# Ternary signs prepared during the offset stage, weights loaded behind the first image, and a first split in four parts

## The chip, the core and the metric

The kernel runs on one core of a Trainium2 chip. The time is device microseconds (us) from start to end. Engines: PE does matmuls (PEld is its weight load), DVE is the vector engine, ACT the scalar engine, POOL is GpSimd, SP issues most of the DMA transfers. PE's clock is granted by a throttle, 1.00 being full. A ratio is the mean time of one kernel's fast runs over that of the other's of the same rounds, so not quite the ratio of the medians that are quoted. Kernels are compared only within the same rounds.

## The reference, cut to what matters

Input is x, two images of 256 channels at 128 x 128, float32.

```python
x = x + L0(group_norm(x))        # three deformable branches, layer norms, GELU, an MLP
x = x + L1(group_norm(x))

def L1(x):                       # weight is (256, 256, 3, 3)
    max_val = max(abs(weight)); w_norm = weight / max_val
    delta = 0.05 * max(abs(w_norm))
    tern = where(w_norm > delta, 1, where(w_norm < -delta, -1, 0))
    wq = where(tern > 0, Wp * tern, where(tern < 0, Wn * tern, tern))
    return conv3x3(x, wq) + bias
```

The ternary weights depend on the inputs alone, not on any result of L0. They can be prepared at any time.

## The kernel before

Four stages follow one another. **Start**: image one is read for its group-norm statistics. **Offset stage** (`phase_a`, 64 groups of four rows over both images): normalise, transpose, convolve to offsets, write interpolation factors (hats). Image two's statistics run beside it. **Sampling stage** with its tail of norms and MLP; it ends with the last store to `x1d`. **Convolution** (`phase_c_signs`): signs in bf16, the image split into three bf16 parts whose sum is the float32 value, 4608 matmuls.

What the change touches:

```python
    def load(name, shape, src):                      # at the very start, 16 loads of weights
        tl = const.tile(shape, F32, name=name)
        nc.sync.dma_start(tl, src)                   # SP issues them before the image
        return tl
    ...
        for b in range(NB):                          # statistics of an image
            for c in range(KC):
                for g0 in range(0, NGRP, XT):
                    xt = ap.tile([P, XT * NG], F32, name="xt", tag="xt", bufs=3)   # ring of three, 1 MB each
                    nc.sync.dma_start(xt, ...)
                    for j in range(XT):
                        nc.vector.bn_stats(...)
            mean, rstd = group_norm(stats, f"gn1_{b}", gps)
            ...
            phase_a(b, ap, psum, k)
    ...
    def quantise(pool, signs=None):                  # in the convolution stage, before its groups
        wq = pool.tile([P, KC, 9, C], F32, ...)
        nc.sync.dma_start(wq, ...)                   # 2304 KB
        nc.vector.tensor_reduce(own, wq, ..., ALU.max, apply_absolute_value=True)
        nc.gpsimd.partition_all_reduce(m, own, ...)
        ...                                          # 13 operations on one column: the thresholds
        for k in range(KC):
            for tap in range(9):
                ts(up, w, pr, ALU.subtract, er, ALU.is_ge)
                ts(dn, w, pr, ALU.add, nc_, ALU.is_le)
                nc.vector.tensor_tensor(signs[:, k, tap, :], up, dn, ALU.subtract)
    ...
    def phase_c_signs(...):
        mean, rstd = group_norm(stats2[b], ...)      # at each image
        for g in range(H // RC):
            ...                                      # xl from x1d; xn normalised; D, four differences of rows
                left = D.rearrange("p i j w -> p (i j) w")
                for i in range(2):
                    part = xc[:, i, k, :, 1 : 1 + W]
                    nc.scalar.copy(part, left)       # 2048 elements at once
                    nc.vector.tensor_tensor(left if i == 0 else xc[:, 2, k, ...], left, part, ALU.subtract)
            for m in range(KC):
                ...                                  # 72 matmuls into four banks, then six DVE additions
```

Names in the profiles: xa is one group's rows of the image, loaded by ACT's queue and normalised by DVE; tpa are its transposes on PE; pz and po are the matmuls that lead to the offsets (offs); parts are the offsets cut into bf16 pieces, which PE transposes (pp) and multiplies to the hats (ph, hb). In the convolution D holds the differences of rows, cring the split image and pc the sums.

Of the kernel before, what the change touches and what calls it, by code (L numbers as in the profile page):

```python
# [9 lines left out]
F32 = mybir.dt.float32  # L10
# [57 lines left out]
def conv_preact_kernel(ctx: ExitStack, tc: tile.TileContext, t: dict, out: bass.AP):  # L68
# [19 lines left out]

    def load(name, shape, src):
        tl = const.tile(shape, F32, name=name)  # L90
        nc.sync.dma_start(tl, src)
        return tl

    gmask = load("gmask", [P, P], t["gmask"])
    convs = [
# [18 lines left out]

    def dram(name, shape):
        return [scratch.tile(shape, F32, name=f"{name}{b}", tag=f"{name}{b}") for b in range(NB)]
# [8 lines left out]
    yd = scratch.tile([3, C, HW], F32, name="yd")  # L125

# [33 lines left out]
    def phase_a(b, pool, psum, k):  # L160
# [160 lines left out]
        for g in range(NGRP):  # L321
            columns(g)
            while G < H // ZG and min(H - 1, G * ZG + ZG - 1 + max(DILS)) < (g + 1) * R:
                parts = offsets(G)
                for j in range(ZG // R):
                    make_hats(G * (ZG // R) + j, parts, j * R)
                G += 1

    with ExitStack() as actx:
# [18 lines left out]
        nc.sync.dma_start(k["wz"], t["wz"].rearrange("(k p) n -> p k n", p=P))  # L348
        nc.sync.dma_start(k["shift"], t["shift"])
        hatw = ap.tile([P, 2, NTAP * NH], F32, name="hatw32")  # L350
        nc.sync.dma_start(hatw, t["hatw"])
        nc.vector.tensor_copy(k["hatw"], hatw)
        pattern = ap.tile([P, NG], F32, name="pattern")
        nc.sync.dma_start(pattern[HALF : HALF + NPAT], t["pattern"])
        for pl in k["planes"]:
            nc.vector.tensor_copy(
                pl[HALF : HALF + NPAT, 1, :], pattern[HALF : HALF + NPAT]
            )
        for parts in k["parts"]:
            nc.vector.memset(parts, 0.0)  # L360
        XT = min(4, NGRP)
        for b in range(NB):
            stats = ap.tile([P, KC, NGRP, 6], F32, name=f"stats1_{b}", tag=f"stats1_{b}")
            for c in range(KC):
                for g0 in range(0, NGRP, XT):
                    xt = ap.tile([P, XT * NG], F32, name="xt", tag="xt", bufs=3)
                    nc.sync.dma_start(
                        xt,
                        x[b, c * P : (c + 1) * P].rearrange("p h w -> p (h w)")[
                            :, g0 * NG : (g0 + XT) * NG  # L370
                        ],
                    )
                    for j in range(XT):
                        nc.vector.bn_stats(stats[:, c, g0 + j, :], xt[:, j * NG : (j + 1) * NG])
            mean, rstd = group_norm(stats, f"gn1_{b}", gps)
            gn1.append((mean, rstd))

            nc.vector.tensor_scalar(negmean[b], mean, -1.0, None, ALU.mult)
            for c in range(KC):
                nc.vector.tensor_scalar(  # L380
                    convs[b][:, c, :], convs[b][:, c, :], rstd[:, c : c + 1], None, ALU.mult
                )
            phase_a(b, ap, psum, k)
# [8 lines left out]
    beyond = nc.values_load(flag[0:1, 0:1], min_val=0, max_val=1)  # L392

# [527 lines left out]
    def quantise(pool, signs=None):  # L921

        wq = pool.tile([P, KC, 9, C], F32, name="wq", tag="wq", bufs=1)
        nc.sync.dma_start(wq, t["l1w"].rearrange("(k p) t o -> p k t o", p=P))
        scale = []
        for name in ("wp", "wn"):
            s = pool.tile([P, 1], F32, name=name, tag=name, bufs=1)
            nc.sync.dma_start(s, t[name].partition_broadcast(P))
            scale.append(s)
        wp, wn = scale  # L930
        nc.vector.tensor_scalar(wn, wn, -1.0, None, ALU.mult)

        def col(name):
            return pool.tile([P, 1], F32, name=name, tag=name, bufs=1)

        own, m, mh, ml, pr, er, z, nc_ = (
            col(f"q_{i}") for i in ("own", "m", "mh", "ml", "pr", "er", "z", "nc")
        )
        nc.vector.tensor_reduce(
            own, wq.rearrange("p k t o -> p (k t o)"), AX.X, ALU.max, apply_absolute_value=True  # L940
        )
        nc.gpsimd.partition_all_reduce(m, own, P, bass.bass_isa.ReduceOp.max)  # L942



        def ts(dst, a, s1, op0, s2=None, op1=None):
            nc.vector.tensor_scalar(dst, a, s1, s2, op0, *(() if op1 is None else (op1,)))

        ts(mh, m, 4097.0, ALU.mult)
        nc.vector.tensor_tensor(ml, mh, m, ALU.subtract)  # L950
        nc.vector.tensor_tensor(mh, mh, ml, ALU.subtract)
        nc.vector.tensor_tensor(ml, m, mh, ALU.subtract)
        ts(pr, m, THR, ALU.mult)
        nc.vector.scalar_tensor_tensor(er, mh, THR_HI, pr, ALU.mult, ALU.subtract)
        nc.vector.scalar_tensor_tensor(er, mh, THR_LO, er, ALU.mult, ALU.add)
        nc.vector.scalar_tensor_tensor(er, ml, THR_HI, er, ALU.mult, ALU.add)
        nc.vector.scalar_tensor_tensor(er, ml, THR_LO, er, ALU.mult, ALU.add)
        nc.vector.scalar_tensor_tensor(er, m, THR_HALF_ULP, er, ALU.mult, ALU.add)

        ts(z, m, 0.0, ALU.is_equal)  # L960
        nc.vector.tensor_tensor(pr, pr, z, ALU.add)
        ts(nc_, er, -1.0, ALU.mult)
        for k in range(KC):
            for tap in range(9):
                w = wq[:, k, tap, :]
                up = pool.tile([P, C], F32, name="up", tag="up", bufs=1)
                ts(up, w, pr, ALU.subtract, er, ALU.is_ge)
                dn = pool.tile([P, C], F32, name="dn", tag="dn", bufs=1)
                ts(dn, w, pr, ALU.add, nc_, ALU.is_le)
                if signs is not None:  # L970
                    nc.vector.tensor_tensor(signs[:, k, tap, :], up, dn, ALU.subtract)  # L971
                    continue
                ts(up, up, wp, ALU.mult)
                nc.vector.scalar_tensor_tensor(w, dn, wn, up, ALU.mult, ALU.add)
        return wq

# [51 lines left out]
    def phase_c_signs(b, pool, psum, cring, signs, sums, wp, half):  # L1028
# [9 lines left out]
        JC = RC // 2  # L1038
        for g in range(H // RC):
# [4 lines left out]
            for k in range(KC):  # L1044
                nc.sync.dma_start(xl[:, k, rows, :], xv[:, k, lo:hi, :])
            xc = cring[g % len(cring)]
            for k in range(KC):
# [16 lines left out]
                left = D.rearrange("p i j w -> p (i j) w")  # L1064
                for i in range(2):
                    part = xc[:, i, k, :, 1 : 1 + W]
                    nc.scalar.copy(part, left)  # L1067
                    nc.vector.tensor_tensor(  # L1068
                        left if i == 0 else xc[:, 2, k, :, 1 : 1 + W], left, part, ALU.subtract
                    )  # L1070
            for m in range(KC):
                pc = psum.tile([P, 4, 512], F32, name="pc", tag="pc", bufs=2)

                for bank, t in ((0, 0), (1, 3), (2, 1), (3, 2)):
# [3 lines left out]
                    for j, (k, kx, i) in enumerate(todo):  # L1078
                        w = (
                            signs[:, k, (t // 3 * 2) * 3 + kx] if t % 3 == 0  # L1080
                            else sums[:, k, t - 1, kx]
# [30 lines left out]

    wpn = small.tile([P, 2], F32, name="wpn", tag="wpn", bufs=1)
    for i, name in enumerate(("wp", "wn")):
        nc.sync.dma_start(wpn[:, i : i + 1], t[name].partition_broadcast(P))
    eq = const.tile([P, 1], I32, name="eq")
    nc.vector.tensor_tensor(eq, wpn[:, 0:1], wpn[:, 1:2], ALU.is_equal)
    same = nc.values_load(eq[0:1, 0:1], min_val=0, max_val=1)

    with tc.If(same > 0) as cmp:  # L1120
        with ExitStack() as cctx:
# [10 lines left out]
            signs = cp.tile([P, KC, 9, C], BF16, name="signs")  # L1132
            quantise(cp, signs)

            sums = cp.tile([P, KC, 2, 3, C], BF16, name="sums")
            for k in range(KC):
                nc.vector.tensor_tensor(
                    sums[:, k, 0], signs[:, k, 0:3], signs[:, k, 6:9], ALU.add
                )
                nc.vector.tensor_tensor(  # L1140
                    sums[:, k, 1], sums[:, k, 0], signs[:, k, 3:6], ALU.subtract
                )
                nc.vector.tensor_tensor(  # L1143
                    sums[:, k, 0], sums[:, k, 0], signs[:, k, 3:6], ALU.add
                )
            half = cp.tile([P, 2], F32, name="half")
            for i in range(2):
                nc.vector.tensor_scalar(
                    half[:, i : i + 1], wpn[:, 0:1], 0.5 - i, None, ALU.mult
                )  # L1150
            for b in range(NB):
                phase_c_signs(b, cp, psum, cring, signs, sums, wpn[:, 0:1], half)
# [102 lines left out]
```

## Time and profile before

| | us |
|---|---|
| median of 3 runs | 7885.2 (7873.1 to 7889.1) |
| span of the profiled execution (timed at 7904.9) | 7903.1 |
| start, to the first pz matmul | 83.5 |
| offset stage, to the last hat (hb) | 874.7 |
| seam, to the first sampling matmul (pm) | 22.4 |
| sampling and tail, to the issue of the last x1d store | 5828.9 |
| convolution, to the end | 1093.6 |

The five stages add up to the span. The lengths come from first and last start times in the views by tile. A hat's end is that of its last DVE operation. From the page of the kernel before: the span; each engine's busy time, share and instruction count; and half of the convolution's matmuls (busy us, mean ns of one, then PE's idle time just ahead of them and what ended most of it).

```profile
span 7903.1 us, 115440 instructions
...
PE 7101.1 (90%) x37984; PEld 5421.9 (69%) x37984; DVE 6400.1 (81%) x13680; ACT 4514.7 (57%) x9350; POOL 715.1 (9%) x1292
...
L1083 PE MATMUL pc<-cring,signs 128*128 128x512 bf16 x2304 | 522.8, 386 | 56.1 <-DVE signs L971 23.6
```

PE is busy for 90% of the span. What a change can take away are the idle stretches, and the last line names one: PE waits in front of the convolution for signs. The shares over the span say nothing of the seams; those are read in the prediction.

### The profile page before, as it was taken

The page shows a single profiled execution, that of the slowest core. Times are in us where ns is not written, and L with a number is a line of the kernel's source. Part 1 is how long each engine was busy: PE and PEld are TensorE (multiplying, and loading weights), DVE is VectorE, ACT ScalarE, POOL GpSimd, SP SyncE. Part 2 cuts the span into 40 slices and gives each one's busy share as a digit, 9 for nine tenths or more (in the row PEclk, how much of TensorE's full clock was granted, in tenths as well). Part 3 has the DMA queues.
Part 4 walks back from the last instruction along what each step waited for, and adds up shares of the span by engine and source line. Part 5 has one row for each costly group of instructions (what it writes and reads, how often), then busy time and mean ns, then how long its engine had stood idle before and what let it go on. Part 6 is the DMA issues. An engine that isn't in the chain of part 4 may idle for free. (4 is left out here: it accounts for less than half of the span.)

```text
span 7903.1 us, 115440 instructions
## 1 busy us (share of the span) xinstructions
PE 7101.1 (90%) x37984; PEld 5421.9 (69%) x37984; DVE 6400.1 (81%) x13680; ACT 4514.7 (57%) x9350; POOL 715.1 (9%) x1292
## 2 busy tenths in 40 slices
PE   5999887899999999899988989999998999699999
PEld 2555577777887777777777777877787777344444
DVE  6666578888999889988688898898889986577776
ACT  1344355666666666667655666666666666333232
POOL 0000000111111111111100111111111111000000
PEclk9999889999999999999999999999999999799999
DMA  8767799999999999998689999999999995222121
GB/s 280 215 187 195 187 229 243 235 247 246 244 240 249 242 243 241 246 243 224 192 233 243 239 248 245 243 240 245 249 240 244 243 242 162 74 74 78 63 82 48
DMA packets 1011327, 1652.66 MB, mean 209 GB/s; under 512 B 120800, under 2 KB 573200, under 8 KB 1006360
## 3 DMA queue, kind: packets, MB, share of 16 engines
q1 hardware_dynamic: 993304, 1611.57, 76.3%
q10 hardware_dynamic: 17408, 33.56, 1.3%
q8 instruction: 304, 4.98, 0.3%
q14 instruction: 311, 2.55, 0.1%
HBM read 1376.69 MB, written 268.09 MB: 208 GB/s over the span
## 5 line engine op out<-in xcount | busy, mean ns | idle before, releaser
L759 PE MATMUL pm<-A,xs 128*128 128x180 f32 (+2 forms) x22288 | 3638.8, 319 | 578.6 <-ACT ev L768 551.2
L759 PEld LDWEIGHTS pm<-A,xs 128*128 128x128 f32 x22288 | 3431.7, 196 | 791.6 <-ACT ev L768 652.0
L768 ACT COPY ev<-pm 128x360 f32<-128x360 f32 (+2 forms) x5572 | 2283.3, 456 | 1517.3 <-DVE ring L733 751.3
L733 DVE SCALAR_TENSOR_TENSOR ring<-ev,defw,ring 128x256 f32<-128x256 f32 (+5 forms) x6272 | 2786.9, 463 | 212.5 <-ACT ev L768 43.2
L689 DVE TENSOR_TENSOR A<-hy,hx 128x768 f32<-128x768 f32 x1130 | 1018.7, 946 | 343.5 <-DMA hx<-hats 170.7
L487 ACT ACTIVATE T<-T,rs 128x256 f32<-128x256 f32 x1280 | 663.8, 595 | 3.3 <-POOL rs L483 3.2
L1083 PE MATMUL pc<-cring,signs 128*128 128x512 bf16 x2304 | 522.8, 386 | 56.1 <-DVE signs L971 23.6
L480 POOL TENSOR_SCALAR rs<-mv 128x4 f32<-128x4 f32 x320 | 108.0, 337 | 5108.0 <-DVE mv L478 4133.9
L1083 PE MATMUL pc<-cring,sums 128*128 128x512 bf16 x2304 | 510.3, 380 | 0.0
L446 PE MATMUL hp<-T,w 128*128 128x512 f32 x1024 | 490.7, 604 | 7.8 <-ACT T L565 7.8
L476 DVE BATCH_NORM_STATS2 st<-T 128x6 f32<-128x256 f32 x1280 | 446.9, 412 | 23.2 <-ACT T L468 23.2
L203 PE MATMUL pz<-wz,xa 128*128 128x486 f32 x1024 | 461.2, 584 | 4.3 <-DVE zr L210 4.3
L1083 PEld LDWEIGHTS <-signs 128*128 128x128 bf16 x2304 | 227.5, 99 | 340.7 <-issue 46.2
L446 PE MATMUL h<-hT,w 128*128 128x512 f32 x1024 | 460.1, 592 | 0.0
L1083 PEld LDWEIGHTS <-sums 128*128 128x128 bf16 x2304 | 225.4, 98 | 274.4 <-DVE sums L1143 0.2
L499 PEld LDWEIGHTS zc<-ident,T 128*128 128x128 f32 x2560 | 342.0, 156 | 98.2 <-issue 61.5
L515 ACT ACTIVATE T<-zc,bb,bw 128x512 f32<-128x512 f32 x384 | 278.5, 779 | 227.8 <-PE zc L499 226.8
L499 PE MATMUL zc<-ident,T 128*128 128x128 f32 x2560 | 384.5, 297 | 19.6 <-ACT T L487 14.1
L1067 ACT CAST cring<-D 128x2048 bf16<-128x2048 f32 x128 | 243.3, 1902 | 222.9 <-PE pc L1083 152.2
L482 POOL TENSOR_TENSOR rs<-rs,mhalf 128x4 f32<-128x4 f32 x320 | 369.6, 1155 | 0.0
L468 ACT COPY T<-tp 128x512 f32<-128x512 f32 x640 | 345.2, 599 | 38.0 <-PE tp L466 37.3
L1091 ACT ACTIVATE o<-xl,l1b 128x1024 f32<-128x1024 f32 x64 | 73.5, 1149 | 506.9 <-DMA out_x<-o 431.7
(120 smaller groups left out, 5768.7 us busy)
## 6 DMA issues: line engine op xcount, KB each, us to landing
hy<-hats SPq DMA_DIRECT2D x1114, 384.0 KB, 6.4
hx<-hats SPq DMA_DIRECT2D x1114, 384.0 KB, 7.3
xs<-table SPq DMA_DIRECT2D x1876, 128.0 KB, 4.4
g12d<-T SPq DMA_DIRECT2D x128, 512.0 KB, 7.1
other<-g12d SPq DMA_DIRECT2D x128, 512.0 KB, 10.1
hats<-hb SPq DMA_DIRECT2D x192, 240.0 KB, 4.3
hats<-hb SPq DMA_DIRECT2D x192, 192.0 KB, 3.3
xl<-x1d SPq DMA_DIRECT2D x56, 640.0 KB, 4.1
```

The lines of the kernel that those rows point to most:

```text
L203: nc.tensor.matmul(pz[:, 0:NZ], lhsT=xt[:, c, r, :], rhs=k["wz"][:, c, :], start=c == 0, stop=c == KC - 1,)
L446: nc.tensor.matmul(out, lhsT=w, rhs=v, start=i == 0, stop=i == n - 1)
L468: nc.scalar.copy(Tv[:, 2 * h : 2 * h + 2, :].rearrange("p j c -> p (j c)"), tp)
L476: pin(nc.vector.bn_stats(st[:, j, :], Tv[:, j, :]))
L482: nc.gpsimd.tensor_tensor(rs[:, 0, :], rs[:, 0, :], mhalf[:, 0:NB4], ALU.pow)
L487: nc.scalar.activation(Tv[:, j, :], Tv[:, j, :], AF.Identity, scale=rs[:, 0, j : j + 1], bias=rs[:, 1, j : j + 1],)
L499: nc.tensor.transpose(zc[:, j * P : (j + 1) * P], Tv[:, j, c * P : (c + 1) * P], ident)
L689: nc.vector.tensor_tensor(dst, hy[:, i0:i1].rearrange("p i t w -> p t i w"), hx[:, i0:i1].rearrange("p i t w -> p t i w"), ALU.mult,)
L733: nc.vector.scalar_tensor_tensor(dst, src, w, dst, ALU.mult, ALU.add)
L759: nc.tensor.matmul(pm[:, j, 0:n], lhsT=xts[b, Rt][T + j][:, c * P : (c + 1) * P], rhs=A[:, m0:m1, AO + (T + j) * CI : AO + (T + j + 1) * C ...
L768: nc.scalar.copy(ev[:, m0:m1, T * CI : (T + 2) * CI].rearrange("p m (t j) -> p t m j", j=CI), pm[:, :, 0:n].rearrange("p t (m j) -> p t m ...
L1083: nc.tensor.matmul(pc[:, bank, :], lhsT=w[:, m * P : (m + 1) * P], rhs=xc[:, i, k, t * JC : (t + 1) * JC, kx : kx + W], start=j == 0, stop ...
```

## The change

Its intent: (1) SP issues the image loads first and the weights behind them; (2) the signs are worked out in small steps among the offset stage's groups, where DVE has idle time, and go to device memory as ready bf16 tiles with their sums; (3) the convolution then only loads them, and its first group is split quarter by quarter so that PE can start on the first bank.

```diff
+    later = []
     def load(name, shape, src):
         tl = const.tile(shape, F32, name=name)
-        nc.sync.dma_start(tl, src)
+        later.append((tl, src))
         return tl
+    def load_now():
+        for tl, src in later:
+            nc.sync.dma_start(tl, src)
+        later.clear()
 ...
+    signd = scratch.tile([P, KC, 15, C], BF16, name="signd")
 ...
+    def store_signs(pool):
+        def chunk(k, i):                  # a piece of the weights, in the ring of image two's statistics
+            w = pool.tile([P, 5, C], F32, name="wk", tag="xt", bufs=3)[...]
+            nc.sync.dma_start(w, ...)
+            return taps, w
+        ...                               # four reductions, then the thresholds
+        for k in range(KC):
+            sg = pool.tile([P, 15, C], BF16, name="sg", tag="xt", bufs=3)
+            for i in range(2):
+                taps, w = chunk(k, i)     # the weights are read a second time
+                for j, tap in enumerate(range(9)[taps]):
+                    up, dn = above(pool, w[:, j, :], limits, sg[:, tap, :])
+                    nc.vector.tensor_tensor(up, up, dn, ALU.subtract)
+                    yield
+            ...                           # three sums
+            nc.sync.dma_start(signd[:, k], sg)
+            yield
 ...
         for g in range(NGRP):
             columns(g)
+            next(beside, None)
 ...
+            if b == 0:
+                load_now()
+                ...                       # wz, shift, hatw, pattern; the last two in the ring of xt
 ...
+            first = b == 0 and g == 0
+            if first:
+                nc.sync.dma_start(signs, signd)
 ...
+                if not first:
+                    split(xc, k, Ds[k], 0, 4)
+            if first:
+                for i in ORDER:
+                    for k in range(KC):
+                        split(xc, k, Ds[k], i, i + 1)
```

The flag that tells whether both scales are equal is read before the sampling stage instead of after it.

## The prediction

> **What bounds the kernel now.** I read the page's slices first, then cut the span with the windows view, then opened the timeline at every seam. The kernel is four stages in a row: loading and statistics of image one (0 to 83 us), the offset stage (83 to 957), sampling with its tail (981 to 6810) and the ternary convolution (6810 to 7903). The change leaves the sampling stage alone, so only the seams and the offset stage matter.
>
> The seam before the convolution, in the windows view (start and end, length, then busy us and instruction count of PE, PEld, DVE, ACT, POOL, then granted clock, DMA share, GB/s):
>
> ```profile
> 6810.00:6820.00 10.00, 1.15 (x4) 1.00 (x4) 5.41 (x25) 0.00 (x0) 0.60 (x1) 0.50 0.77 284
> 6820.00:6830.00 10.00, 0.00 (x0) 0.00 (x0) 6.95 (x10) 3.44 (x3) 0.47 (x2) 0.50 0.89 353
> 6830.00:6840.00 10.00, 2.02 (x4) 0.54 (x5) 10.00 (x24) 3.80 (x2) 0.00 (x0) 0.50 0.47 163
> 6840.00:6850.00 10.00, 5.98 (x14) 1.92 (x13) 10.00 (x18) 3.80 (x2) 0.00 (x0) 0.65 0.00 0
> 6850.00:6860.00 10.00, 0.00 (x0) 0.00 (x0) 10.00 (x17) 3.09 (x2) 0.00 (x0) 0.52 0.00 0
> 6860.00:6870.00 10.00, 4.95 (x12) 1.57 (x13) 10.00 (x21) 2.62 (x2) 0.00 (x0) 0.50 0.01 2
> ...
> 7000.00:7100.00 100.00, 100.00 (x463) 45.10 (x461) 76.53 (x85) 31.20 (x20) 0.00 (x0) 1.00 0.21 77
> ```
>
> From 6830 to 6880 DVE is full and PE starves at half clock; from 6887 PE is full, 463 matmuls in 100 us, 0.216 us each. So DVE sets this seam and PE the rest. The timeline there:
>
> ```profile
> 6812.63 0.38 SPq L924 DMA_DIRECT2D wq<-in_l1w  x1
> ...
> 6821.29 4.95 DVE L939 TENSOR_REDUCE q_own<-wq 128x1 f32<-128x4608 f32 x1 [1.96 <-DMA wq<-in_l1w]
> ...
> 6837.12 1.01 PE L1083 MATMUL pc<-cring,signs 128*128 128x512 bf16 x2 [17.99 <-DMA xl<-x1d]
> ...
> 6865.01 10.99 PE L1083 MATMUL pc<-cring,signs 128*128 128x512 bf16 x36 [17.68 <-DVE signs L971]
> ```
>
> The weights' load, their reduction and the signs (L971) come in front of the matmuls, and DVE interleaves them with the splits of later groups. When sums become usable (6886.85), 69 of 4608 matmuls are done, 15 us of work. So the convolution behaves as if it had started at 6886.85 - 15 = 6872 at full rate, 59 us after the sampling stage's last store landed (6812.6).
>
> The seam at the start:
>
> ```profile
> 17.34 48.86 SPq L367 DMA_DIRECT2D xt<-in_x  x16
> ...
> 25.12 7.33 DVE L374 BATCH_NORM_STATS2 stats<-xt 128x6 f32<-128x512 f32 x12 [0.92 <-DMA xt<-in_x]
> ...
> 83.53 7.55 PE L203 MATMUL pz<-wz,xa 128*128 128x486 f32 x16
> ```
>
> Twenty-odd weight loads are issued on SP before the first image load, at 17.34. DVE ends the last statistic at 76.45; normalisation starts at 81.14.
>
> The offset stage is PE-bound: 616.6 of 623 us busy from 310 to 933, DVE at 402.4 (65%), so DVE has about a third free. From 80 to 310 PE is busy for only 204 of 230. There, image two's statistics run beside, and a late load blocks DVE's queue:
>
> ```profile
> 162.35 0.55 DVE L154 TENSOR_SCALAR xa<-xa,gn_mean,gn_rstd 128x512 f32<-128x512 f32 x1 [5.18 <-DMA xa<-in_x]
> ...
> 164.33 0.29 PE L290 MATMUL pp<-ident_b,parts 128*128 128x128 bf16 x1 [5.07 <-DVE parts L280]
> ```
>
> **What the Trainium skill says.** "TensorE: Matmul & The Clock Gate", What's actually happening: the array idles at half rate and reaches full rate only after about 3.4 us of sustained work. The trace agrees: the 14 matmuls at 6841 took 0.427 us each, the steady ones 0.216. "VectorE: DVE Perf Modes", The TRN2 errata: each operation pays a fixed time, so many small ones cost more than one large. Here an L1068 of 2048 elements takes 2.285 us and a subtraction of 512 takes 0.683, so four cost 0.45 us more by durations, and about nothing from start to start (0.60). "DMA: Bandwidth & Descriptors", Issuing engines are not separate DMA queues: loads from ACT and SP share the same 16 engines. The 5.18 us wait above, for an ACT-issued load while SP loads image two, agrees.
>
> **The change, part by part.**
>
> Convolution seam. Off the path come the 2304 KB weight load, its 4.95 us reduction, the all-reduce, some 13 threshold operations at 0.15, 36 comparisons at 0.40, 18 subtractions at 0.41 and 6 sums at 0.55: 5 + 2 + 14.4 + 7.4 + 3.3 = 32 us of DVE, and the wait. Added: one load of 128 x 15,360 bytes = 1920 KB of ready signs, behind the first two image loads. The new path from 6812.6:
> - The group norm stays: aggregates, two tiny matmuls and the power end near 6820.2 (the variance is ready at 6819.3, the power takes 0.7).
> - xl (576 KB each, 3.9 us to landing) is there by 6817.5. The signs, scaled from the 8.6 us that 2304 KB took, land near 6821. So the transfer hides behind the group norm.
> - DVE then has two normalisations (0.87), two row memsets (0.17), eight D operations and sixteen quarter subtractions at 0.60 to 0.62: 1.7 + 0.3 + 5.0 + 9.8 = 16.8 us, to about 6837. PE begins once the first quarter of channel half 0 is split, near 6825, and follows DVE quarter by quarter; at half clock for the first 3.4 us, it ends the first 72 matmuls (15.5 us when fed) near 6842. An equivalent start of 6842 - 15.5 = 6826.5.
> - The next group needs 16 us of DVE (1.9 + 5 + 4 x 2.29) and the first output's six additions (4.1): ready at 6857, when PE ends its second 72. No large stall, but no slack. As DVE's queue before was filled with later groups' work in every gap, I add 4.5 us.
>
> Equivalent start 6831 against 6872: **41 us gained**. Later stalls, such as the pause at image two (7370 to 7400, about 20 us), stay.
>
> Start seam. The image loads can issue at about 2.3 instead of 17.34: 15 us. They are limited by their ring of three (16 x 1 MB in 59 us, SP waiting for DVE and for landings), not by bandwidth, so the statistics move by the same 15, and the last ends near 61.5. What takes back some of it: the weights now issue after the sixteenth image load (about 51), need about 14 us of SP's time as before (1.2 to 15.4), then wz lands near 69 where the normalised data would be ready at 67. The cast of hatw (lands about 72) sits in DVE's in-order queue and may come in front of the normalisation. I take 4 back: **11 us gained**.
>
> Offset stage. It receives those 32 us of DVE, in pieces under 1.5 us, over some 25 of 64 groups: 1.3 us for each 13.6 us group, where DVE has 4.5 idle. So it hides. But the weights are read twice (4608 KB) and signs stored (1920 KB): 6.7 MB beside the 16.8 MB of image two's statistics, whose stage loses 26 us of PE. In proportion that would be 10 us more. The sign pieces take image two's buffers (the same ring of three), so the two spread out rather than add. I take half: **5 us lost**. The flag's register load moves to the seam at 957: 0.5 lost.
>
> Sum: 41 + 11 - 5 - 0.5 = 46.5; 7885.2 - 46.5 = 7838.7, say **7839 us**.
>
> **The rivals.**
> (a) DVE work moved into the offset stage lands on PE's path. For: any DVE wait there (a weight piece still in flight, the all-reduce, 2.6 us from the reduction's end to its use before) holds up the normalisation and evacuations behind it, as at 162 us, and each pause costs the clock ramp too. Against: 35% of DVE idle, and image two's first aggregate is needed only some 250 us after it is done (254.75). Four such pauses more cost 30 us: 7865.
> (b) At the convolution's start the split chain replaces the signs: DVE fills ACT's waits with 2.29 us subtractions of later groups. Each quarter then waits; the gain falls to 28 us: 7852.
> (c) The start gains nothing, as wz, hatw or shift becomes the last to arrive: 7850. Against: the DMA is only 53 to 80% busy from 50 to 80 us, so there is room.
> (d) All hides and both seams are ideal (45 + 15): 7826.
> None reaches 2%, which is 158 us; both seams together are 75 us of PE idleness and 83 us of preparation that must mostly stay.
>
> **Range and chances.** Single terms are uncertain by 7 (convolution), 5 (start), 8 (offset stage), and the long sampling stage may shift by some 10 as data moves in device memory (three runs before differ by 16). Roots of squares: about 15 for one standard deviation. So 7820 to 7862 for 8 in 10. Faster by over 2% or slower by over 2%: 1% each, the latter for a mishap in the instruction order.
>
> **What would show it.** Right: first convolution matmul 12 to 16 us after the last x1d store lands, no quantise line there, clock full within 20 us; first xt issue near 2 us and first pz matmul near 72; the offset stage from first pz to last ph matmul within 874 +0 to +12 us; the sampling stage unchanged in length. Wrong: PE waiting for hatw or wz after the statistics, DVE waiting for weight pieces with PE behind it, the offset stage longer by 20 or more, PE waits for cring of over 10 us in the first two groups, or a sampling stage that differs by over 15 us.

## The result, and the profile after

The changed kernel took 7849.1 us in the median (7846.3 to 7850.3, 4 runs), against 7882.2 (7873.1 to 7889.1, 4 runs) for the kernel before: ratio 0.9958, 95% interval 0.9941 to 0.9975. The gain by means is 33 us where 46.5 were forecast; the time lies within the stated range.

From the page of the changed kernel, the lines that answer to those above:

```profile
span 7847.5 us, 115488 instructions
...
PE 7102.5 (91%) x37984; PEld 5435.0 (69%) x37984; DVE 6397.7 (82%) x13695; ACT 4523.2 (58%) x9362; POOL 720.6 (9%) x1292
...
L1167 PE MATMUL pc<-cring,signs 128*128 128x512 bf16 x4608 | 1007.5, 382 | 20.0 <-ACT cring L1114 12.8
```

The work is the same; the span shrank. The wait for signs is gone from the matmuls' line, and the two groups of matmuls are one.

**The convolution's seam.** The windows view of the changed kernel (start and end, length, busy us and count of PE, PEld, DVE, ACT, POOL, granted clock, DMA share, GB/s), then its timeline (start, length, engine, line, what). The last store is issued at 6795.34 here:

```profile
6800.00:6810.00 10.00, 1.73 (x5) 1.14 (x6) 8.37 (x20) 3.18 (x5) 0.70 (x1) 0.50 0.99 384
6810.00:6820.00 10.00, 6.98 (x18) 2.41 (x18) 10.00 (x17) 8.67 (x14) 0.00 (x0) 0.54 0.79 315
6820.00:6830.00 10.00, 10.00 (x47) 4.50 (x46) 10.00 (x14) 2.73 (x3) 0.00 (x0) 1.00 0.00 0
6830.00:6840.00 10.00, 10.00 (x48) 4.52 (x47) 9.96 (x12) 4.25 (x3) 0.00 (x0) 1.00 0.13 52
```

```profile
6798.42 1.14 SPq L1125 DMA_DIRECT2D xl<-x1d  x2
...
6799.69 0.34 SPq L1128 DMA_DIRECT2D signs<-signd  x1
...
6809.32 0.59 PE L1167 MATMUL pc<-cring,signs 128*128 128x512 bf16 x1 [4.65 <-DMA signs<-signd]
...
6813.61 66.68 PE L1167 MATMUL pc<-cring,signs 128*128 128x512 bf16 x294 [1.08 <-DVE cring L1115]
```

PE starts in earnest 18 us after the last store was issued, and from 6820 it is full at full clock. The run of 294 matmuls has no stop in it and is cut only by the end of the view: with the two before it, it holds the first two groups (144 each) and the start of the third. The signs arrive 9.6 us after their issue (6809.3). The group norm had ended at 6805.7 and the first piece of the split at 6808.0, so they were not quite hidden; but PE then waits for the split (cring), which sets the start of the long run.

**The start.** The changed kernel's timeline:

```profile
2.11 44.60 SPq L475 DMA_DIRECT2D xt<-in_x  x16
...
34.07 19.84 DVE L482 BATCH_NORM_STATS2 stats<-xt 128x6 f32<-128x512 f32 x32
...
57.86 0.43 SPq L485 DMA_DIRECT2D wz<-in_wz  x1
...
59.24 5.45 PE L306 MATMUL tpa<-ident,xa 128*128 128x128 f32 x24 [2.21 <-issue]
64.53 27.90 PE L320 MATMUL pz<-wz,xa 128*128 128x486 f32 x68
```

The kernel before, same place:

```profile
81.78 1.95 PE L189 MATMUL tpa<-ident,xa 128*128 128x128 f32 x8 [2.20 <-issue]
```

The last statistic ends at 53.9 (76.5 before), the first pz matmul starts at 64.5 (83.5 before). PE records no wait for wz, issued at 57.9. It runs 24 transposes ahead of its first pz matmul where the kernel before runs 8. Counted to the first transpose, the start came 22.5 us earlier (59.2 against 81.8), 5.3 us after the last statistic in both. All profiles with the weights behind the image have the 24, all others the 8, so the stage lengths below, cut at the first pz matmul, book some 3.5 us of the same work as start in the former and as offset stage in the latter.

**The offset stage.** Three lines of the changed kernel's timeline. A load of xa is issued by ACT at 218.5, DVE waits for it, and PE waits for the parts cast that stands behind DVE's wait:

```profile
218.53 0.37 ACTq L296 DMA_DIRECT2D xa<-in_x  x1
...
229.47 0.55 DVE L173 TENSOR_SCALAR xa<-xa,gn_mean,gn_rstd 128x512 f32<-128x512 f32 x1 [7.04 <-DMA xa<-in_x]
...
231.34 0.29 PE L407 MATMUL pp<-ident_b,parts 128*128 128x128 bf16 x1 [7.16 <-DVE parts L397]
```

This load took 10.9 us from issue to use (229.47 - 218.53); the DMA view of the kernel before gives 4.9 as the median from issue to landing. It is the pattern that the prediction showed at 162 us, and there is more of it: from 85 to 400 us DVE waits for xa 41.9 us in total (37.3 in the second profile), against 33.8 (30.3) before. Over the whole stage PE stood idle for 47.8 us (45.3), against 33.5 (29.9). Image two's statistics and the signs, each with the first and last start, by tile: first the kernel before, then the changed one.

```profile
L374 DVE BATCH_NORM_STATS2 stats<-xt x128: 667/677/696, 25.1 to 254.0; 128x6 f32<-128x512 f32 x128
```

```profile
L482 DVE BATCH_NORM_STATS2 stats<-xt x128: 634/676/696, 12.1 to 367.3; 128x6 f32<-128x512 f32 x128
...
L215 DVE TENSOR_SCALAR sg<-wk,q_pr,q_er x18: 397/404/413, 113.6 to 185.6; 128x256 bf16<-128x256 f32 x18
```

The signs were not spread over 25 groups at one step each, as the program text reads. The scheduler pulled them forward, to 95 to 198 us, and image two's statistics, which share the ring of three, moved behind them and ended 113 us later.

The best ruler of this stage is the time from one offset step to the next (a step is eight rows, two groups). It is 25.6 us when PE never waits. Worked out from the start times of the copy of po, steps 1 to 12:

```
step                  1     2     3     4     5     6     7     8     9    10    11    12
before             27.3  35.1  34.4  37.5  26.7  26.3  25.6  25.6  25.7  25.6  25.7  25.6
changed            23.6  30.4  29.4  30.4  36.0  33.1  35.2  27.6  32.7  26.0  25.6  25.6
changed, 2nd       23.4  27.9  30.1  26.6  36.7  33.1  38.2  31.0  33.5  26.9  25.6  25.7
```

In these profiles the slow steps last about as long as image two's statistics do: to step 4 before, to step 9 after. It is not a rule: in e3 below, without signs, the statistics ended at 250 us, but the steps were slow (27.7 to 32.6) up to step 8, at 348 us. Steps 1 to 12 together took 341 us before (335 in the second profile, 341 in e3) and 356 (359) after.

**By stages.** All profiles, in us, cut as in the table above. Labels are those of the experiments.

```
                          start  offset   seam  sampling  convolution    span
before                     83.5   874.7   22.4    5828.9       1093.6   7903.1
e1 before again            81.7   866.5   22.4    5828.1       1094.1   7892.8
changed                    64.5   880.2   25.6    5825.0       1052.2   7847.5
e2 changed again           64.8   886.4   23.7    5822.9       1050.1   7847.9
e3 start only              68.8   868.0   21.7    5829.9       1093.5   7881.9
e4 signs, no start         86.8   884.9   23.4    5830.0       1050.3   7875.4
e5 DVE work only           63.7   872.4   24.6    5815.4       1050.4   7826.5
e6 loads only              64.5   887.4   23.3    5821.1       1052.0   7848.3
e7 late signs              64.7   873.9   23.7    5819.9       1052.1   7834.3
e8 no quarters             64.3   876.8   25.2    5831.4       1054.6   7852.3
e9 late, both norms        67.0   871.9   25.5    5824.3       1030.5   7819.2
e10 five xa buffers        65.3   872.1   24.9    5815.4       1052.2   7829.9
e11 late flag              64.9   894.1   24.2    5819.1       1050.4   7852.7
e12 e9 with five           65.8   872.3   25.3    5821.3       1029.1   7813.8
```

Taking both profiles of each kernel: start +18.0 us, offset stage -12.7, seam -2.3, sampling +4.6, convolution +42.7, together 50.3. The rounds say 33 and 42. Part of the difference is scatter: the runs of the kernel before reach from 7872 to 7913 us, and both of its profiled executions lie in the upper part. The sampling stage alone, whose instruction lists are the same in all 14 profiles, reaches from 5815 to 5831 us, and nothing in these runs says why. So one profile's total is no measure of a change of 10 us; stage lengths are the better guide.

### The profile page after: what moved, and what is told of

Same layout as the page of the kernel before. It is cut to its first block, busy times and chain, and to the rows that moved or that the text cites. A ratio compares the mean times of both kernels' runs of the same rounds, so it can differ in the third digit from the quotient of the medians.

```text
span 7847.5 us, 115488 instructions
## 1 busy us (share of the span) xinstructions
PE 7102.5 (91%) x37984; PEld 5435.0 (69%) x37984; DVE 6397.7 (82%) x13695; ACT 4523.2 (58%) x9362; POOL 720.6 (9%) x1292
## 5 line engine op out<-in xcount | busy, mean ns | idle before, releaser
L1167 PE MATMUL pc<-cring,signs 128*128 128x512 bf16 x4608 | 1007.5, 382 | 20.0 <-ACT cring L1114 12.8
L1167 PEld LDWEIGHTS <-signs 128*128 128x128 bf16 x4608 | 452.4, 98 | 574.5 <-issue 30.1
L853 DVE TENSOR_SCALAR ring<-ev,defw 128x256 f32<-128x256 f32 (+1 forms) x788 | 265.6, 338 | 105.7 <-ACT ev L892 105.2
L1114 ACT CAST cring<-D 128x2048 bf16<-128x2048 f32 (+1 forms) x140 | 245.0, 1755 | 184.4 <-PE pc L1167 126.7
L570 PEld LDWEIGHTS h<-hT,w 128*128 128x128 f32 x1024 | 189.1, 190 | 186.6 <-issue 186.1
```

Of the source, the lines that this page charges most:

```text
L570: nc.tensor.matmul(out, lhsT=w, rhs=v, start=i == 0, stop=i == n - 1)
L1167: nc.tensor.matmul(pc[:, bank, :], lhsT=w[:, m * P : (m + 1) * P], rhs=xc[:, i, k, t * JC : (t + 1) * JC, kx : kx + W], start=j == 0, stop ...
```

## The experiments

Theory T: the seams give what the prediction said, and the offset stage takes some back because the weight pieces and stores travel, and take slots of the ring, while image two's statistics are loaded. Rival D: DVE's added work delays PE. Besides, the first profiles left 20 us between the stage sums and the medians, which needed a second profile.

### e1 and e2: both kernels again

No edit.

> The kernel before, unchanged, for a second profile of it. Cut by the seams, the two profiles at hand differ by 19.0 us at the start (first pz matmul at 83.5 and 64.5), -5.5 in the offset stage, -3.1 at the seam behind it, +4.2 in sampling and +41.1 at the convolution: 55.7 together, yet the medians differ by only 33. Theory A (the profiled execution of before was slow by chance, in the sampling stage): this profile shows first pz matmul at 83.5 +-1, the convolution's end 59 + 1022 us after the last x1d store as before, and a sampling stage (first pm matmul to last x1d store landed) near 5810 instead of 5832, at a total near 7882. Rival B (the seams themselves vary from run to run): sampling within 4 us of 5832 and a seam that is shorter by 10 or more. Timing ratio 1.000 +-0.001.

Measured: 7893.6 us in the median (7884.9 to 7912.8, 6 runs), ratio 1.0002 (0.9988 to 1.0016). Sampling took 5828.1 us to the last store's issue, so this profile gives my Theory A, a shorter sampling stage in ordinary runs of the kernel before, no support; but the profiled run, at 7894.6, is not one of the short runs near 7882 that it was about. Rival B got its sampling stage right and its seam wrong: no seam was shorter by 10 us. The offset stage was 8 us shorter than in the first profile, the other stages within 2 us.

> The changed kernel, unchanged, for its second profile and more rounds. Total 7849 +-4, 33 us below before (ratio 0.9958). Theory A': its sampling stage is truly longer than that of before on average, 5828 +-4 against some 5810, so this profile repeats 5828. Rival: its sampling stage scatters by 15 us as that of before does, so it lies outside 5820 to 5836. Seams as in the first profile within 1 us: first pz matmul at 64.5, convolution's first long run of matmuls 15.5 us after the last store landed.

Measured: 7853.4 us (7842.2 to 7864.5, 6 runs), ratio 0.9947 (0.9934 to 0.9959): by means 42 us below the 11 runs of before, where 33 were expected. The sampling stage repeated within 2.1 us. It is not longer than before; nothing is given back there. The instruction lists of PE, DVE, ACT and SP in the sampling stage are the same in both kernels. The missing microseconds were most likely scatter together with the offset stage, which is longer in both profiles of the changed kernel (880.2, 886.4) than in both of before (874.7, 866.5).

### e3: the start alone

```diff
 (kernel before)
-        nc.sync.dma_start(tl, src)
+        later.append((tl, src))      # issued behind image one's loads, with wz, shift, hatw, pattern
```

> The kernel before with only its weights' loads moved behind the first image's loads; signs and splits untouched. Additive seams: first pz matmul near 64.5 and a total of 7882 - 19 = 7863. If whatever is given back comes from a shift of the sampling stage in time or from the offset stage's start, it shows here too: 7868 to 7882. If it comes from the signs' traffic or from the new buffer in device memory, this kernel gains its whole 19 us.

Measured: 7880.8 us (7870.2 to 7885.9, 5 runs), ratio 0.9979 (0.9966 to 0.9992), by means 15 us gained, not the 19 of additive seams. The first pz matmul came at 68.8, not 64.5, and the offset stage kept the length it has without signs (868.0). So this part gains 13 to 15 us and nothing of it is given back later.

### e4: the signs alone

```diff
 (changed kernel)
-        later.append((tl, src))
+        nc.sync.dma_start(tl, src)   # and wz, shift, hatw, pattern ahead of image one's loads again
```

> The changed kernel with the weights loaded ahead of the first image again (signs among the groups, four-part split kept). Additive seams: the convolution's 41 us less 5.5 in the offset stage and some 3 behind it, 7882 - 32 = 7850; if 18 us are given back in sampling because of the new buffer in device memory: 7868; if the give-back belongs to the earlier start: 7850.

Measured: 7876.1 us (7869.3 to 7878.7, 5 runs), ratio 0.9972 (0.9959 to 0.9985), by means 21 us gained, not 32. The table says where: the convolution gave its 43 us; the offset stage took 884.9, which is 14 more than the mean of the two profiles of before (870.6); and the start came at 86.8, 4 us later than their mean, with the two scales now also ahead of the image in SP's queue (first image load at 19.05) and hatw and pattern in slots of the images' ring. The gains of e3 and e4 add up to 36 us, those of the whole change are 42; the intervals allow that the parts simply add.

### e5 and e6: the signs' DVE work or their traffic

```diff
 (e5: no weight pieces; the work is done on resident tiles; in the text the result is stored after the stage)
-            nc.sync.dma_start(w, ...)
-                up, dn = above(pool, w[:, j, :], limits, sg[:, tap, :])
+                up, dn = above(pool, zero, limits, sg[:, tap, :])
 (e6: all pieces and stores, but one tiny copy in place of the comparisons; no sums, reductions of 8 elements)
-                up, dn = above(pool, w[:, j, :], limits, sg[:, tap, :])
-                nc.vector.tensor_tensor(up, up, dn, ALU.subtract)
+                nc.vector.tensor_copy(sg[:, tap, 0:1], w[:, j, 0:1])
```

Their outputs are wrong, which doesn't matter for the times.

> The changed kernel with the signs' DVE work left in place but on resident tiles: no weight pieces are loaded and the result is stored only at the end of the stage, so no traffic and no slot of image two's ring is taken. The result is wrong on purpose. In the two profiles of each so far the offset stage (first pz matmul to last hb) took 866 to 875 us without the signs' work and 880 to 886 with it; PE waits there for the parts cast, which stands behind a normalisation that waits for its xa load. Theory T (traffic: the 6.7 MB and the shared ring lengthen the time in which xa loads come late): stage back to 866 to 875, image two's last statistic before 270. Rival D (DVE's 32 us of work delay PE): stage stays at 880 to 887, since the same DVE operations are there.

Measured: offset stage 872.4; total 7829.9 us (7827.2 to 7836.3, 4 runs), ratio 0.9922 (0.9906 to 0.9939).

> The changed kernel with all eight weight pieces and both stores, in the same ring, but with the comparisons, subtractions, sums and full reductions taken out (one tiny DVE operation for each piece keeps the buffers' order). The result is wrong on purpose. Theory T (traffic and ring): stage stays at 878 to 887. Rival D (DVE work): 866 to 875. If both halves cost, about 875 to 880 in this one and the one before.

Measured: offset stage 887.4; total 7850.8 us (7839.8 to 7852.5, 4 runs), ratio 0.9943 (0.9926 to 0.9960).

Image two's statistics by tile, in e5 and then in e6:

```profile
L485 DVE BATCH_NORM_STATS2 stats<-xt x128: 636/676/697, 12.2 to 290.1; 128x6 f32<-128x512 f32 x128
```

```profile
L478 DVE BATCH_NORM_STATS2 stats<-xt x128: 634/676/695, 12.2 to 334.1; 128x6 f32<-128x512 f32 x128
```

The DVE work without traffic leaves the stage at the length it has without signs. The traffic without the DVE work costs it all. So Theory T holds, and Rival D falls as the main cause. The totals say the same: e5 is 18 us below e6 by means in the same rounds. (In e5 the statistics still ended at 290, not before 270; that expectation was missed.)

Two limits. Steps 1 to 12 took 349 us in e5 and 359 in e6, against 335 to 341 without signs and 356 to 359 in the changed kernel: with one profile each, a share of some us for the DVE work isn't excluded. And e5 is not wholly without traffic: the scheduler issued its stores at 324 to 329 us, inside the stage but behind the statistics. Pieces in flight and slots taken from the ring were never tried apart, so which of the two costs more stays open.

### e7: the same traffic behind image two's statistics

```diff
 (changed kernel)
-            next(beside, None)
+            if b == NB - 1:
+                next(beside, None)
```

> The changed kernel with the signs' steps moved from image one's groups to image two's, so that they come behind image two's statistics in the ring. Theory T in its ring form: the statistics end near 255 to 265 as before the change, the sign pieces then meet a DMA load of only 0.7, and the offset stage takes 868 to 876, a total of 10 us below the changed kernel (ratio to before 0.9935). Rival (any extra traffic costs its share wherever it comes): the stage stays at 880 and the total at 0.9947.

Measured: offset stage 873.9; total 7839.6 us (7818.2 to 7850.9, 6 runs), ratio 0.9930 (0.9914 to 0.9946). The scheduler again pulled the steps forward, but now they queue in the ring behind the statistics, by tile:

```profile
L483 DVE BATCH_NORM_STATS2 stats<-xt x128: 635/676/697, 12.2 to 241.7; 128x6 f32<-128x512 f32 x128
```

The statistics end at 242 instead of 367, and the stage is 9 us shorter than the mean of the changed kernel's two profiles (883.3). So the same bytes cost less when they do not meet the statistics. e9 below repeats it with 871.9; the five profiles with the signs among image one's groups and four xa buffers lie between 876.8 and 894.1. They are not free, though: beside and just behind the sign pieces (302 to 424 us) steps 8, 9, 11 and 12 took 32.6, 33.7, 29.4 and 29.8 us. The ratios (0.9930, against 0.9943 for e8) point the same way; their intervals overlap, so the total alone doesn't prove it.

### e8: the first split whole

```diff
-                if not first:
-                    split(xc, k, Ds[k], 0, 4)
-            if first:
-                for i in ORDER:
-                    for k in range(KC):
-                        split(xc, k, Ds[k], i, i + 1)
+                split(xc, k, Ds[k], 0, 4)
```

> The changed kernel with the first group's split whole again instead of in four parts. By durations the whole chain for the first group is cast 1.90, subtraction 2.29, cast 1.90, subtraction 2.29 for each channel half, the halves overlapping: the third part of the second half is ready about 11 to 13 us after the first D, where the quarters let PE start in earnest 7 us after it (6806.7 to 6813.6). So the first long run of matmuls starts 4 to 8 us later and the total rises by 3 to 8 us (7853 if the changed kernel has 7849). Rival (the quarters are worth nothing, as the second group sets the pace): total unchanged within 2 us.

Measured: total 7851.0 us (7842.1 to 7854.4, 4 runs), ratio 0.9943 (0.9927 to 0.9960), not separable from the changed kernel. PE in the timeline of e8, whose last store was issued at 6797.7 (span less convolution):

```profile
6817.83 1.01 PE L1162 MATMUL pc<-cring,signs 128*128 128x512 bf16 x2 [3.31 <-ACT cring L1114]
6820.16 30.09 PE L1162 MATMUL pc<-cring,signs 128*128 128x512 bf16 x125 [1.32 <-DVE cring L1115]
```

The long run starts 22.5 us after the store, 4 later than with quarters (18.3), and the convolution is 2.4 to 4.5 us longer in the stage table. By these profiles, one of e8, the four-part split is worth some 3 us out of the 43; the totals do not show it.

### e9: late signs, and both group norms ahead of the convolution

In every profile so far PE stops at the change of image in the convolution. In the windows view of the kernel before, around that point:

```profile
7370.00:7400.00 30.00, 12.92 (x45) 5.34 (x44) 26.32 (x36) 10.65 (x6) 0.74 (x1) 0.66 0.18 62
```

Only 45 matmuls ran in 30 us, where 139 fit. The two matmuls of image two's group norm stand in PE's queue behind all of image one's (the first starts at 7371.71, as image one's last run ends), so nothing of image two is normalised before PE is through: the first of its rows at 7378.

```diff
 (e7)
+            gn2 = [group_norm(stats2[b], f"gn2s_{b}", ...) for b in range(NB)]
             for b in range(NB):
-                phase_c_signs(b, cp, psum, cring, signs, wpn[:, 0:1])     # group norm inside
+                phase_c_signs(b, cp, psum, cring, signs, wpn[:, 0:1], *gn2[b])
```

> The late signs of the run before, and both images' second group norms worked out ahead of the convolution instead of one at each image. In all profiles PE idles at the change of image there (7370 to 7400 in the kernel before, some 20 us of matmul time lost), because image two's group norm has its two tiny matmuls in PE's in-order queue behind all of image one's. Theory: that pause goes, the last pc matmul comes 1022 us after the last x1d store instead of 1041, and the total is 7839 - 18 = 7821 (ratio 0.9908). Rival: the pause has another cause too (buffers of the first group, evacuation), and less than 8 us go.

Measured: 7814.6 us (7807.4 to 7834.1, 5 runs), ratio 0.9899 (0.9885 to 0.9914). The convolution took 1030.5 us, 21.6 less than in e7. The windows view of e9 around the change of image shows no stop:

```profile
7300.00:7350.00 50.00, 50.00 (x232) 22.47 (x231) 34.35 (x37) 17.47 (x11) 0.00 (x0) 1.00 0.24 89
```

This correct version is about 1% faster than the kernel before, and faster than the changed one (0.9947).

### e10: a fifth xa buffer

```diff
-            xt = pool.tile([P, KC, R, W], F32, name="xa", tag="xa", bufs=4)
+            xt = pool.tile([P, KC, R, W], F32, name="xa", tag="xa", bufs=5)
```

> The changed kernel with five buffers instead of four for xa, so that each load can be issued a group (13 us) earlier. If late xa loads are what PE pays for beside the statistics, most of the pauses over 25.7 us between two offset steps go: the stage takes 855 to 870 instead of 880 to 886, total 7849 - 16 = 7833. If the loads are issued when ACT's own queue reaches them, and not when a buffer is free, nothing changes: 880 to 886.

Measured: offset stage 872.1, total 7842.9 us (7831.7 to 7856.8, 4 runs), ratio 0.9939 (0.9924 to 0.9954). The stage came out 11 us shorter than the changed kernel's mean, just outside what was expected, but the ratio doesn't differ from that of e11 of the same rounds (0.9941). One profile and overlapping totals: it points to late loads, but settles nothing.

### e11: the flag read late

```diff
-    same = nc.values_load(eq[0:1, 0:1], min_val=0, max_val=1)      # ahead of the sampling stage
+    same = nc.values_load(eq[0:1, 0:1], min_val=0, max_val=1)      # ahead of the convolution
     with tc.If(same > 0) as cmp:
```

> The changed kernel with the flag for equal scales read where it was read before, after the sampling stage, instead of ahead of it. The seam from the last hb to the first pm matmul was 22.4, 22.4 and 21.7 us in the three profiles with the late read and 23.3 to 25.6 in the six with the early one. If the read is the cause: 21.5 to 22.5 here. If not (the last stores of the hats land later, or chance): 23.3 to 25.6. Total within 3 us of 7849 either way; the convolution's start, 18 us after the last store, unchanged within 1 us.

Measured: seam 24.2 us, total 7849.0 us (7848.0 to 7854.5, 4 runs), ratio 0.9941 (0.9925 to 0.9956). The flag's read is not what lengthens the seam by some 2 us; the cause of that stays open. The offset stage of this run took 894.1, the longest of all, which shows how much it scatters when signs and statistics meet.

### e12: e9 with the fifth buffer

The edit is that of e10, on e9.

> The version of e9 (late signs, both second group norms ahead of the convolution) with five xa buffers as in e10. If the two savings in the offset stage are of one kind (fewer xa loads that come late) they overlap: the stage takes 865 to 872 and the total lies 0 to 8 us below that of e9, ratio to before 0.989 to 0.990. If they add, the stage takes 855 to 865 and the ratio is 0.988.

Measured: 7815.8 us (7809.5 to 7823.8, 4 runs), ratio 0.9914 (0.9897 to 0.9931), offset stage 872.3. The stage is that of e9 (871.9) and the ratio lies outside both expectations, in another call than e9's. The fifth buffer adds nothing measurable to e9; whether it saves anything alone, e10 left open.

## Why the prediction was right

The time lay in its range, at 7849 against 7839, but two of its four terms were off, by some 7 and 9 us in opposite directions, and partly cancelled: that much of the agreement is luck. By its own steps:

- **Convolution seam, 41 us: right.** The stage shrank by 42.7. The signs' transfer hid behind the group norm and the first splits, PE began its long run 18 us after the last store's issue, and the second group cost no stall. Rival (b), splits that replace the signs, did not happen. By the prediction's own measure: 296 matmuls were done at 6880.3, 64 us of work at the steady rate, so PE behaved as if it had started some 18 us after the last store landed (6798.4); the forecast was 18.4, its 4.5 us for fillers included.
- **Start seam, 11 us: mis-sized, measured 18 in the whole change and 13 to 15 alone (e3).** The step that failed was "the statistics move by the same 15". The statistics also ran faster: from the first to the end of the last 41.8 us (12.1 to 53.9) instead of 51.3 (25.1 to 76.5), with DVE almost without waits. The give-back of 4 us only seems to fit: from the last statistic to the first pz matmul it took 10.6 us instead of 7.1, but neither wz nor hatw held PE up. It ran 24 transposes instead of 8 first, work that the offset stage would have had; to the first transpose it took 5.3 us in both. So nothing was given back. Why the loads ran faster, and why e3 got less of it than the changed kernel, no run isolates.
- **Offset stage, 5 us: mis-sized, measured 13 to 15** (16 when counted from the first transpose). The two profiles of each kernel differ by 12.7. With all profiles of the same kind the lengths are 880.2, 886.4, 884.9, 876.8 and 894.1 with the signs among image one's groups, and 874.7, 866.5 and 868.0 without them: means 884.5 and 869.7. The step that failed was "the two spread out rather than add; I take half". Sharing the ring did spread them, but late xa loads stopped DVE, and then PE, for longer in total (PE idle for 47.8 and 45.3 us of the stage, against 33.5 and 29.9). The estimate in proportion to the bytes, 10 us, was the better one and still low. That DVE's 32 us would mostly hide was right (e5).
- **Flag, 0.5 us: wrong in its cause.** The seam grew by 2.3 us, but moving the read back did not shorten it (e11).
- **Rival (a)** had the path right (a wait in DVE's queue with PE behind it, with the granted clock at 0.87 from 220 to 310 us, where PE paused most, against 1.00 from 500 to 700) and the trigger wrong: DVE waited for xa, not for weight pieces or for the all-reduce. In the changed kernel's waits from 85 to 400 us, DVE waits for xa 41.9 us in total, for weight pieces 4.5.

Of the signs it named for being right, the first image load at 2.1 us, the missing quantise lines, the sampling stage (4 to 6 us shorter) and the offset stage (880.2 and 886.4, within 874 + 12) came true. The first pz matmul came at 64.5 and not 72, and the first pc matmul 10.9 us after the last store landed and not 12 to 16.

What the first rounds could not tell, 33 or 42 us, stays a matter of scatter: the means of the kernel before run from 7882 to 7895.

## What to carry to other kernels

Work that depends on inputs alone belongs ahead of the stage that needs it, but ask what its transfers will meet there: idle time of an engine is no room for DMA, and a ring shared with another stream delays that stream. Look where a scheduler really puts such work, since the program text does not say. And an engine that is the bound should get the small matmuls of the next phase (here a group norm, worth over 20 us) before the long run, not behind it.

## What the Trainium skill lacked or had wrong

- "DMA: Bandwidth & Descriptors", Issuing engines are not separate DMA queues, says that the time to initiate a DMA is usually small beside the DMA itself. For one DMA that agrees here (most took 0.33 to 0.56 us of SP's queue), but it lacks what a row of them costs. In the kernel before, the 20 ahead of the image held SP's queue from 0.74 to 17.34 us, 6.9 us of it SP's own waits for earlier loads, and the change of this order alone gained 13 to 15 us (e3).
- The same section says that transfers from all queues interleave on the same 16 engines; no page gives a figure for how much longer one such load then takes. Here a 512 KB load took 10.9 us from issue to use beside others, against a median of 4.9 to landing in the kernel before.
